# Reciprocal roots as a power on GpSimd, the B matrices on ScalarE, and another hand-made order

## The chip, the cores and the metric

The kernel runs on one core of one Trainium2 chip. Its engines work at the same time, each through its own instructions in order: TensorE (PE, with its weight loads as PEld), VectorE (DVE), ScalarE (ACT), GpSimd (POOL) and SyncE (SP), which issues the DMA transfers here. The metric is the device time of one execution in microseconds; the median of several executions is compared.

## The reference

Input is x, 16 sequences of 256 tokens of 128 values, in fp32. Four layers follow one another, each added to x after a layer norm: a Mamba layer (A), a two-deep attention-and-feed block (F), a state-space layer (C), and the same block F again with the same weights.

```python
def _layernorm(x, axis=-1, eps=1e-05):
    m = jnp.mean(x, axis=axis, keepdims=True)
    v = jnp.var(x, axis=axis, keepdims=True)
    return (x - m) / jnp.sqrt(v + eps)
...
    x = x + _L0_attn_a_ref(_layernorm(x, axis=-1), ...)   # A: conv, SSD scan, y * rsqrt(mean(y*y) + 1e-05)
    x = x + _L0_ffn_ref(_layernorm(x, axis=-1), ...)      # F
    x = x + _L0_attn_b_ref(_layernorm(x, axis=-1), ...)   # C
    x = x + _L0_ffn_ref(_layernorm(x, axis=-1), ...)      # F
```

In F, each of two depths projects q, k and v, scales q and k to length one (`t / jnp.clip(jnp.linalg.norm(t, axis=-1, keepdims=True), 1e-12)`, in 8 heads of 64), rotates them, attends in windows of 64 tokens to the own and the preceding window, projects, and then runs a layer norm and a gated feed-forward net. In C, for each of 16 states s, a recurrence runs along the tokens:

```python
        def step(state, inp):
            Ab, Bb, Bt, xt, Ct = inp
            state = Ab * state + Bb * Bt[:, None, :] * xt[:, :, None]
            out = jnp.einsum('bds,bs->bd', state, Ct)
            return (state, out)
```

followed by a layer norm of `out * z` and a projection.

## The kernel before

**Groups and stages.** Two sequences form a group (512 tokens, 4 tiles of 128), so there are 8 groups, and each goes through the stages A, F, C, F. A group's work in a stage is a unit, or six units in F: two attentions and one feed for each of two depths. In `stage` and `run` each unit gets an age, 8 times the stage plus the group, plus a little within F. In the profile below, A fills about the first 330 us, the first F runs to about 940, C to about 1600, and the second F to the end, with overlap at the borders.

**Order.** No engine's order is that of the code. A `Recorder` stands in for the machine: `add` puts each instruction of `mamba`, `attention`, `feed` and `ssm` into a `Node` with a modelled length from `lengths` and with its dependences from `touch`. `order` then plays the whole program through with these lengths: on each engine, of the nodes that could start within a small slack, it takes the one with the lowest rank. The rank is the unit's age plus the unit's entry in the table `LATE`. At most 20 units are open (6 of A, 4 of C). `order` also models table loads on ACT, a lock between POOL and some DVE instructions (`pool_end`, `both_end`), the switch of PE between tile forms (`quad`), the granted clock of PE (`HAM`, `RISE`, `FALL`), and it plans `fill` matmuls on `identb` where PE would stand still. `emit` writes the program in that order, so that each engine's order is fixed before the run.

**Buffers** come from pools (`POOLS`): 8 PSUM banks (`ps`), 47 tiles of 128x512 fp32 (`k2`) and others. A bank is taken by `mm`.

**Reciprocal roots.** `rsqrt` serves two callers. `ln_stats` calls it with `add=eps` for each layer norm, and `mamba` once more for its own norm: 96 calls in all, for 2 or 4 columns of 128 rows. They go to `rsqrt_bank`, which works on DVE in a PSUM bank: a first guess from the bits of the number, then two steps of refinement, 16 instructions, each depending on the one before or the one before that. `attention` calls `rsqrt` with `floor=1e-24` for the lengths of q and k, 32 columns, 64 calls; this is the same method in 12 POOL instructions on the tiles `rnv`, `rny`, `rnq` and `rnu`. The results go to `normalize` (DVE), to `normalize_all` (DVE for `nb`, ACT for the tiles) and, in attention, to `rotary`, which multiplies `ra` by them on POOL ahead of PE's transposes.

**The loop over states in C.** For each s of 16, `ssm` makes a matrix `b_M` for each of the group's four tiles: `self.two`, which has ones on two diagonals, times the column B of that s, a scale for each row. POOL makes all four in one instruction of 128x512, into a ring of two tiles. The row of C goes from DRAM to all partitions by an SP DMA into a ring of three (`b_r`). For each half c of the channels, ACT makes the decay by a tanh into a ring of four (`b_z`), PE multiplies `b_uT` by `b_M` into a bank, DVE adds the carry and scans along the tokens, POOL multiplies by `b_r`, and PE transposes the product and adds it up in `py`:

```python
            M = ring("b_M", s, 2, [P, NT, P])
            nc.gpsimd.tensor_tensor(M, self.two.unsqueeze(1).broadcast_to([P, NT, P]), Bt[:, :, s:s + 1].broadcast_to([P, NT, P]),
                                    ALU.mult)
```

All instructions are emitted in `emit` (L530, fillers L528), so the profile is read by tile names and not by lines. Where it says `root`, it is `rsqrt_bank`; `sm` and `pr` are the softmax, `ss` the lengths, `po` the projections.

Of the kernel before, what the change touches and what calls it, by code (L numbers as in the profile page):

```python
# [13 lines left out]
F32 = mybir.dt.float32  # L14
# [8 lines left out]
P = 128  # L23
# [18 lines left out]
NEG = -1.0e30  # L42
HCH = ((0, 128), (128, 128), (256, HID - 256))

ROWS = 3


# [3 lines left out]
       "sv": 0.08, "sg": 0.08, "gg": 0.083, "gt": 0.055, "gv": 0.035, "gs": 0.035}  # L51
TABLES = {AF.Exp: "e", AF.Tanh: "e", AF.Ln: "l", AF.Gelu: "g"}
SLOW = (AF.Tanh, AF.Ln, AF.Gelu)
HAM = 3.413
RISE, FALL = 0.53, 0.29
FILL = 0.2
POOL_SLOW = ("a_am", "a_MT", "b_av")

LATE = (1.71, -0.25, -0.97, -1.58, -0.56, 0.05, 0.77, -0.02, 1.32, 0.12, 1.03, 0.48, 0.04, 0.73, -3.9, -0.04, -1.0, -0.43, 0.8, -0.1,
        0.74, -0.48, -0.42, -1.22, 0.46, 0.57, -1.43, -1.37, -0.89, 0.25, -0.32, -0.13, -0.0, 0.04, 0.01, 0.43, -0.54, -0.18, -0.08,  # L60
        0.42, 1.15, 0.41, -0.76, -0.23, -1.37, 0.12, 0.15, -0.13, -0.45, -0.06, 0.15, 0.32, -1.79, -3.79, -1.6, 0.9, 0.04, -1.73,
        -0.17, 0.72, 0.47, 0.54, 0.44, -0.76, -0.42, 0.07, -0.71, 1.79, 1.36, 0.48, 1.05, -5.16, -2.95, 0.43, 1.03, 2.12, -0.17,
        -1.16, 0.54, 0.74, -1.96, 2.0, -0.03, 1.01, -0.93, -0.9, 1.24, 1.4, 1.4, 1.52, 2.58, 1.42, -1.22, 0.27, 2.16, 1.92, 0.34,
        -2.92, 3.73, 3.74, 1.92, 1.18, 1.54, 0.45, -1.45, 1.62, 0.87, -1.92, 0.62, -2.4, 1.87, 0.44, -1.58, -4.05, -0.49, -3.33, 2.98)
LIMIT = {"A": 6, "C": 4}
WINDOW = 20
SLACK = {"tensor": 0.0, "vector": 0.1, "scalar": 0.1, "gpsimd": 0.1, "sync": 0.0}
# [2 lines left out]
def lengths(eng, op, outs, ins, kw):  # L70

    free = lambda r: int(np.prod(r.shape[1:]))
    n = max(free(r) for r in outs + ins)
    if eng == "tensor":
        n = free(outs[0])
        if op == "transpose" or kw.get("is_transpose"):
            occ = 0.106
        elif ins[0].dt == F32:
            occ = 2 * max(0.111 * free(ins[0]) / P, 0.00084 * n)
        else:  # L80
            occ = max(0.111, 0.000452 * n)
        return occ, occ + 0.22
    aps = sum(isinstance(kw.get(k), Ref) for k in ("bias", "scale"))
    if eng == "scalar":
        occ = 0.1 + 0.000714 * n + 0.09 * aps + 0.05 * (kw.get("func") in SLOW) + 0.065 * ("accum_out" in kw)
        if outs[0].t.cls == "hT":
            occ += 0.1
        return occ, occ + 0.12
    if eng == "vector":
        n1 = n * (2 if op == "tensor_tensor_scan" else 1)  # L90
        small = sum(free(r) == 1 for r in ins) if n > 1 else 0
        two = op in ("tensor_scalar", "tensor_copy", "memset") and not any(r.t.cls == "ps" for r in outs + ins)
        occ = 0.06 + 0.00104 * n1 * (0.5 if two else 1.0) + 0.05 * small
        if outs[0].t.cls == "hT":
            occ += 0.1
        return occ, occ + 0.09
    if eng == "gpsimd":
        full = op == "tensor_tensor" and not any(r.wide for r in ins)
        per = 0.00226 if full else 0.00182 if op == "tensor_tensor" else 0.0009
        occ = 0.14 + per * n if n < 256 else 0.06 + per * n  # L100
        if outs[0].t.name.startswith(POOL_SLOW):
            occ += 0.2
        return occ, occ + 0.07
    return 0.06, 2.3


def sem(a, b):
# [71 lines left out]

class Node:  # L180
    __slots__ = ("eng", "calls", "occ", "lat", "pre", "post", "wait", "unit", "i", "table", "bufs", "new", "start", "ready", "both",
                 "quad", "fill", "took", "flow")

    def __init__(self, eng, unit, i):
        self.eng, self.unit, self.i = eng, unit, i
        self.calls, self.occ, self.lat, self.pre, self.post, self.bufs, self.new = [], 0.0, 0.0, {}, [], [], []
        self.table, self.both, self.quad, self.start, self.flow = None, False, False, None, 0.0


class Unit:  # L190
# [13 lines left out]
class Recorder:  # L204
# [10 lines left out]
        self.unit = Unit(name, age)  # L215

    @contextmanager
    def burst(self, quad=False):

        self.open = self.node("tensor")  # L220
        self.open.quad = quad
        yield
        self.open = None
# [13 lines left out]
    def add(self, eng, op, args, kw):  # L237
# [27 lines left out]
        elif eng == "tensor" and outs[0].shape[0] == 64:  # L265
            occ, lat = 0.55 * occ, 0.55 * occ + 0.22
        if eng == "tensor":
            q.flow += (2 if ins[0].dt == F32 and op == "matmul" and not kw.get("is_transpose") else 1) * int(np.prod(outs[0].shape[1:])) / 2400
        q.lat = q.occ + lat
        q.occ += occ  # L270
# [72 lines left out]
    def order(self, slack, rank, window):  # L343
# [8 lines left out]
        free = {c: [(0.0, i) for i in range(n)] for c, n in self.pools.items()}  # L352
        oldest = 0
        at = {e: 0.0 for e in self.ENGINES}
        table, quad, pool_end, both_end = None, False, 0.0, 0.0

        half, stretch, work = True, 0, 0.0
        cands = {e: [] for e in self.ENGINES}
# [78 lines left out]
        while len(done) < len(self.nodes):  # L437
# [11 lines left out]
            if e == "tensor":  # L449

                idle = t - at[e]
                bank = max((free[b.cls][0][0] for b in q.new if b.cls == "ps"), default=None)
                if FILL and idle > FILL and bank is not None and q.unit.age > -1:
                    q.fill = max(0, int((t - max(bank, at[e])) / (0.43 if half else 0.215)))
                    work += q.fill * (0.43 if half else 0.215)
                if bool(q.quad) != quad:
                    quad = bool(q.quad)
                    t += 0.09 if quad else 0.16
                while t > (stretch + 1) * HAM:
                    half = work < (RISE if half else FALL) * HAM  # L460
                    work, stretch = 0.0, stretch + 1
                if half:
                    occ, lat = 2.05 * occ, lat + 1.05 * occ
                work += q.flow * (2 if half else 1)
            if q.table:
                table = q.table
# [4 lines left out]
                pool_end = t + lat  # L471
                dirty.add("vector")
            if q.both:
                both_end = t + lat
                dirty.add("gpsimd")
            for b in q.new:
                b.place = free[b.cls].pop(0)[1]
# [39 lines left out]

    def emit(self, nc, make, idle):
        self.prepare()
        late = dict(zip(self.units, LATE))  # L520
        nodes, end = self.order(SLACK, lambda q: q.unit.age + late[q.unit], WINDOW)
        for q in nodes:
            for b in q.new:
                b.real = make(b)
# [99 lines left out]
class Kern:  # L624
# [75 lines left out]

    def rsqrt(self, x, n, tag, add=None, floor=None):


        g = self.nc.gpsimd
        k1, c1 = 0.7039522, 2.3892446
        if add is not None:
            return self.rsqrt_bank(x, n, add)
        v, y, q, u = (self.t([P, n], tag=f"{tag}{i}") for i in "vyqu")
        g.tensor_scalar(v, x, floor, None, ALU.max)
        g.tensor_scalar(y.bitcast(I32), v.bitcast(I32), -0.5, float(0x5F1FFFF9), ALU.mult, ALU.add)  # L710
        g.tensor_tensor(q, y, y, ALU.mult)
        g.tensor_tensor(q, q, v, ALU.mult)
        g.tensor_scalar(q, q, -k1, k1 * c1, ALU.mult, ALU.add)
        g.tensor_tensor(y, y, q, ALU.mult)
        g.tensor_tensor(q, y, y, ALU.mult)
        g.tensor_tensor(q, q, v, ALU.mult)
        g.tensor_scalar(u, q, 0.375, -1.25, ALU.mult, ALU.add)
        g.tensor_tensor(u, u, q, ALU.mult)
        g.tensor_scalar(u, u, 1.875, None, ALU.add)
        g.tensor_tensor(y, y, u, ALU.mult)  # L720
        return y

    def rsqrt_bank(self, x, n, add):

        g = self.nc.vector
        k1, c1 = 0.7039522, 2.3892446
        bank = self.mm("root")
        e, y, q = (bank[:, i * n:i * n + n] for i in range(3))
        v, u, r = (self.t([P, n], tag="root") for i in range(3))
        k = lambda value: self.number(value).broadcast_to([P, n])  # L730
        self.nc.after_last()
        g.memset(e, add)
        g.tensor_tensor(v, x, e, ALU.add)
        g.tensor_tensor(e, x, e, ALU.add)
        g.tensor_tensor(q, e.bitcast(I32), k(-0.5), ALU.mult)
        g.tensor_tensor(y.bitcast(I32), q, k(float(0x5F1FFFF9)), ALU.add)
        g.tensor_tensor(u, y, v, ALU.mult)
        g.tensor_tensor(q, u, y, ALU.mult)
        g.tensor_tensor(u, k(c1), q, ALU.subtract)
        g.tensor_tensor(y, y, u, ALU.mult)  # L740

        g.tensor_tensor(u, y, v, ALU.mult)
        g.tensor_tensor(q, u, y, ALU.mult)
        g.tensor_tensor(u, q, k(10 / 3 / k1 ** 2), ALU.subtract)
        g.tensor_tensor(q, u, q, ALU.mult)
        g.tensor_tensor(u, q, k(5 / k1 ** 4), ALU.add)
        g.tensor_tensor(y, y, u, ALU.mult)
        g.tensor_tensor(r, y, k(0.375 * k1 ** 5), ALU.mult)
        return r

    def number(self, value):

# [523 lines left out]
    def ssm(self, g):  # L1276
# [86 lines left out]

        for s in range(16):
            M = ring("b_M", s, 2, [P, NT, P])
            nc.gpsimd.tensor_tensor(M, self.two.unsqueeze(1).broadcast_to([P, NT, P]), Bt[:, :, s:s + 1].broadcast_to([P, NT, P]),
                                    ALU.mult)
            q = ring("b_r", s, ROWS, [P, n])
            nc.sync.dma_start(q, rows[s, :].partition_broadcast(P))
            for c in range(2):  # L1370
# [120 lines left out]
```

## Time and profile before

| | us |
|---|---|
| median of 3 runs | 2267.78 |
| range of the runs | 2260.32 to 2270.0 |
| profiled execution | 2273.8 |
| span of the profiled execution | 2272.0 |
| PE busy | 2104.1 |
| DVE busy | 1819.0 |
| POOL busy | 1642.7 |
| ACT busy | 1545.5 |
| filler matmuls on PE, busy | 147.07 |
| table loads on ACT, 84 of 1.283 us | 107.8 |

The mean granted clock of PE is 0.955 of full speed. The span is that from the first to the last instruction of the profiled execution; 1.8 us lie around it. Busy shares are means over stages that differ, so they are read by stretch. A wait is put down to the instruction that came last before the waiting one could start. The chain of waits goes back from the last instruction, at each step to what released it.

The costliest groups of POOL, as the page has them (line, engine, operation, out<-in, shapes, count | busy us, mean ns | idle before it, and what ended most of it):

```profile
L530 POOL TENSOR_TENSOR ra<-ra,rb 128x512 f32<-128x512 f32 x256 | 327.8, 1284 | 126.1 <-DVE rb L530 62.8
L530 POOL TENSOR_TENSOR b_z<-b_z,b_r 128x512 f32<-128x512 f32 x256 | 323.3, 1285 | 34.2 <-DVE b_z L530 10.6
L530 POOL TENSOR_TENSOR pr<-pr,sm 128x512 f32<-128x512 f32 x256 | 265.6, 1045 | 112.8 <-DVE sm L530 60.0
```

### The profile page before, as it was taken

Reading aid. Unit: us, or ns where it says so; the run is one execution under the profiler, and the core shown is the slowest. Engines: PE = TensorE matmul, PEld = TensorE weight load, DVE = VectorE, ACT = ScalarE, POOL = GpSimd, SP = SyncE. Lnnn points to the kernel's source line nnn. Section 1 sums busy time; section 2 is a strip of 40 time slices with the busy share of each in tenths; the row PEclk is TensorE's granted clock in tenths of the full one; section 3 lists DMA queues with packets and bytes.
Section 4 is the critical chain, followed back from the end, with each engine's and each line's share of the span. In section 5 each row is a group of like instructions: output and inputs, shape, how many; then the busy total and the mean of one; then the engine's idle time right before and its main releaser. Section 6 shows DMA issues by size and latency. Waiting matters only on the chain.

```text
span 2272.0 us, 56516 instructions
## 1 busy us (share of the span) xinstructions
PE 2104.1 (93%) x20190; PEld 1704.8 (75%) x20190; DVE 1819.0 (80%) x5840; ACT 1545.5 (68%) x4155; POOL 1642.7 (72%) x2180
## 2 busy tenths in 40 slices
PE   8899899999999999989898988899999999999999
PEld 5667567777787678778797777888777787778777
DVE  7777699877787896585999798889888859785865
ACT  5526137878778688866655756566687777879685
POOL 2424438895877695758897969988986968977593
PEclk8768799999999999999999989999999999999999
DMA  3000011000110110111221212222100101010001
GB/s 114 21 20 10 15 40 25 20 16 23 36 27 16 34 30 20 28 39 41 85 83 59 86 58 72 64 70 66 34 23 11 32 17 31 18 29 12 20 20 25
DMA packets 56520, 84.60 MB, mean 37 GB/s; under 512 B 15280, under 2 KB 20528, under 8 KB 56240
## 3 DMA queue, kind: packets, MB, share of 16 engines
q1 hardware_dynamic: 56240, 80.99, 12.5%
q8 instruction: 161, 2.64, 0.5%
q14 instruction: 119, 0.97, 0.1%
HBM read 55.53 MB, written 8.65 MB: 28 GB/s over the span
## 4 chain that ended last, share of the span: by engine, by line
PE 50%; DVE 24%; POOL 16%; ACT 6%; issue 4%; DMA 1%; SPq 0%; POOLq 0%; DVEq 0%; ACTq 0%
PE mm L530 31%; POOL ra L530 7%; PE po L530 6%; DVE b_z L530 5%; PE av L530 4%; PE sc L530 3%; PE py L530 3%; POOL pr L530 3%; DVE root L530 3%; ACT pr L530 2%; DVE rb L530 2%; DVE ra L530 2%; PE mm L528 2%; POOL b_z L530 2%; DVE ss L530 2%
## 5 line engine op out<-in xcount | busy, mean ns | idle before, releaser
L530 POOL TENSOR_TENSOR ra<-ra,rb 128x512 f32<-128x512 f32 x256 | 327.8, 1284 | 126.1 <-DVE rb L530 62.8
L530 ACT ACTIVATE pr<-sc,nm 128x128 f32<-128x128 f32 x1024 | 365.8, 395 | 32.5 <-DVE nm L530 27.8
L530 POOL TENSOR_TENSOR b_z<-b_z,b_r 128x512 f32<-128x512 f32 x256 | 323.3, 1285 | 34.2 <-DVE b_z L530 10.6
L530 POOL TENSOR_TENSOR pr<-pr,sm 128x512 f32<-128x512 f32 x256 | 265.6, 1045 | 112.8 <-DVE sm L530 60.0
L530 DVE TENSOR_TENSOR_SCAN b_z<-mm,b_z 128x256 f32<-128x256 f32 x512 | 323.4, 675 | 11.7 <-ACT b_z L530 4.2
L530 PE MATMUL mm<-b_M,b_uT 128*128 128x128 f32 x2048 | 267.1, 281 | 19.3 <-DVE mm L530 5.6
L530 ACT ACTIVATE b_z<-b_ld,b_A 128x512 f32<-128x512 f32 x256 | 178.6, 720 | 150.1 <-PE py L530 129.5
L530 PEld LDWEIGHTS mm<-b_M,b_uT 128*128 128x128 f32 x2048 | 248.5, 195 | 30.3 <-POOL b_M L530 9.4
L530 POOL TENSOR_TENSOR ra<-ra,rny 128x512 f32<-128x512 f32 x256 | 260.8, 1044 | 2.5
L530 ACT ACTIVATION_READ_ACCUMULATOR pr<-sc,nm 128x1 f32 x1024 | 239.1, 234 | 0.0
L530 DVE TENSOR_REDUCE nm<-sc 128x4 f32<-128x512 f32 x256 | 165.5, 681 | 59.1 <-PE sc L530 58.1
L530 DVE TENSOR_TENSOR rb<-mm,tab 128x256 f32<-128x256 f32 x512 | 194.9, 413 | 0.1
L530 DVE TENSOR_TENSOR ra<-mm,tab 128x512 f32<-128x512 f32 x256 | 174.2, 681 | 22.6 <-ACT sq L530 19.7
L530 ACT ACTIVATE sq<-mm 128x512 f32<-128x512 f32 x256 | 153.0, 614 | 49.7 <-PE mm L530 41.2
L530 PE MATMUL py<-ident,b_z 128*128 128x128 f32 x1024 | 157.5, 280 | 31.1 <-POOL b_z L530 30.3
L530 DVE TENSOR_REDUCE ss<-sq 128x8 f32<-128x512 f32 x256 | 172.2, 674 | 0.0
L530 PE MATMUL mm<-ident,pr 128*128 128x128 f32 x1024 | 153.2, 280 | 19.0 <-POOL pr L530 14.0
L530 PE MATMUL mm<-ident,ra 128*128 128x128 f32 x1024 | 152.6, 283 | 19.6 <-POOL ra L530 16.1
L530 ACT COPY pT<-mm 128x512 f32<-128x512 f32 x256 | 147.5, 610 | 32.0 <-PE mm L530 28.6
L530 POOL TENSOR_TENSOR b_M<-b_two,b_CB 128x512 f32<-128x512 f32 x128 | 133.8, 1055 | 31.9 <-PE mm L530 31.7
L530 PEld LDWEIGHTS py<-ident,b_z 128*128 128x128 f32 x1024 | 116.7, 142 | 52.2 <-POOL b_z L530 47.4
L530 PEld LDWEIGHTS mm<-ident,pr 128*128 128x128 f32 x1024 | 113.7, 141 | 55.7 <-POOL pr L530 39.6
(295 smaller groups left out, 5501.2 us busy)
## 6 DMA issues: line engine op xcount, KB each, us to landing
b_r<-b_rows SPq DMA_DIRECT2D x128, 256.0 KB, 3.3
v<-v SPq DMA_DIRECT2D x128, 128.0 KB, 2.2
x<-xd SPq DMA_DIRECT2D x32, 256.0 KB, 2.8
xd<-x SPq DMA_DIRECT2D x24, 256.0 KB, 2.0
x<-in_x_dram SPq DMA_DIRECT2D x16, 256.0 KB, 2.8
x<-xd SPq DMA_DIRECT2D x32, 128.0 KB, 2.4
out_dram<-x SPq DMA_DIRECT2D x16, 128.0 KB, 2.1
w<-in_wqkv_dram SPq DMA_DIRECT2D x6, 256.0 KB, 5.3
```

Source lines behind the costliest of these rows:

```text
L528: self.tc.keep_in_program_order(nc.tensor.matmul(bank[:, 0:512], idle[0], idle[1], start=True, stop=True))
L530: r = getattr(e, op)(*(a.get() if isinstance(a, Ref) else a for a in args), **{k: v.get() if isinstance(v, Ref) else v for k, v in kw.item ...
```

## The change

Three things change.

1. `rsqrt` becomes two POOL instructions for either caller: an addition (or, in attention, the maximum with the floor) and a power with exponent -0.5, both operands as tensors where the exponent is a broadcast constant. `rsqrt_bank` is gone, and with it its DVE instructions and its PSUM banks. The layer-norm roots move from DVE to POOL.
2. In `ssm`, `b_M` is made by ACT instead of POOL: four activations of 128x128 (`Identity`, with the column of B as the scale) for one POOL instruction of 128x512. `M_ACT = 4` makes the condition hold for every s.
3. The order: the modelled lengths in `lengths` change a little, PE's switch times become a table by kind of switch, some matmuls get an extra length, the lock's end is modelled otherwise, and the rank gets a second part. `LATE` has a new entry for each unit, and after these an entry for each kind of node (stage, engine and first tile name), which is added too.

The diff, with the numbers of `LATE` and some of the bookkeeping left out:

```diff
+M_ACT = 4
...
+TENSOR_SLOW = ("a_B", "a_st")
+SWITCH = {(0, 4): 0.09, (0, 2): 0.09, (4, 0): 0.16, (2, 0): 0.16, (2, 4): 0.14, (4, 2): 0.09}
 HAM = 3.413
-RISE, FALL = 0.53, 0.29
+RISE, FALL = 0.51, 0.275
...
     if eng == "scalar":
-        occ = 0.1 + 0.000714 * n + 0.09 * aps + 0.05 * (kw.get("func") in SLOW) + 0.065 * ("accum_out" in kw)
+        occ = 0.106 + 0.000714 * n + 0.09 * aps + 0.05 * (kw.get("func") in SLOW) + 0.065 * ("accum_out" in kw)
...
-        occ = 0.06 + 0.00104 * n1 * (0.5 if two else 1.0) + 0.05 * small
+        occ = 0.065 + 0.00104 * n1 * (0.5 if two else 1.0) + 0.05 * small
+        if two and small:
+            occ += 0.03
...
-        occ = 0.14 + per * n if n < 256 else 0.06 + per * n
+        occ = 0.15 + per * n if n < 256 else 0.068 + per * n
         if outs[0].t.name.startswith(POOL_SLOW):
-            occ += 0.2
+            occ += 0.1
...
+def kind(q):
+
+    return q.unit.name[0] + q.eng[0] + next(a.t.name for a in q.calls[0][1] if isinstance(a, Ref)).rstrip("0123456789")
...
+            if len(q.calls) == 0 and ins[0].t.name.startswith(TENSOR_SLOW):
+                occ, lat = occ + 0.16, lat + 0.16
+            q.slow |= ins[0].dt == F32 and not q.quad
...
-                if bool(q.quad) != quad:
-                    quad = bool(q.quad)
-                    t += 0.09 if quad else 0.16
+                if q.quad != quad:
+                    t += SWITCH[quad, q.quad]
+                    quad = q.quad
...
                 if half:
-                    occ, lat = 2.05 * occ, lat + 1.05 * occ
+                    occ, lat = 2.05 * occ, lat + 1.05 * (lat if q.slow else occ)
...
             if q.both:
-                both_end = t + lat
+                both_end = t + occ - 0.01
...
-        late = dict(zip(self.units, LATE))
-        nodes, end = self.order(SLACK, lambda q: q.unit.age + late[q.unit], WINDOW)
+        late, kinds = dict(zip(self.units, LATE)), {}
+        for q in self.nodes:
+            q.rank = q.unit.age + late[q.unit] + LATE[len(self.units) + kinds.setdefault(kind(q), len(kinds))]
+        nodes, end = self.order(SLACK, lambda q: q.rank, WINDOW)
...
     def rsqrt(self, x, n, tag, add=None, floor=None):
 
-
         g = self.nc.gpsimd
-        k1, c1 = 0.7039522, 2.3892446
+        v, y = (self.t([P, n], tag=f"{tag}{i}") for i in "vy")
+        k = lambda value: self.number(value).broadcast_to([P, n])
         if add is not None:
-            return self.rsqrt_bank(x, n, add)
-        v, y, q, u = (self.t([P, n], tag=f"{tag}{i}") for i in "vyqu")
-        g.tensor_scalar(v, x, floor, None, ALU.max)
-        g.tensor_scalar(y.bitcast(I32), v.bitcast(I32), -0.5, float(0x5F1FFFF9), ALU.mult, ALU.add)
...
-        g.tensor_tensor(y, y, u, ALU.mult)
+            g.tensor_tensor(v, x, k(add), ALU.add)
+        else:
+            g.tensor_scalar(v, x, floor, None, ALU.max)
+        g.tensor_tensor(y, v, k(-0.5), ALU.pow)
         return y
-
-    def rsqrt_bank(self, x, n, add):
-
-        g = self.nc.vector
...
         for s in range(16):
             M = ring("b_M", s, 2, [P, NT, P])
-            nc.gpsimd.tensor_tensor(M, self.two.unsqueeze(1).broadcast_to([P, NT, P]), Bt[:, :, s:s + 1].broadcast_to([P, NT, P]),
-                                    ALU.mult)
+            if s % 4 < M_ACT:
+                for i in range(NT):
+                    nc.scalar.activation(M[:, i, :], self.two, AF.Identity, scale=Bt[:, i, s:s + 1])
+            else:
+                nc.gpsimd.tensor_tensor(M, self.two.unsqueeze(1).broadcast_to([P, NT, P]), Bt[:, :, s:s + 1].broadcast_to([P, NT, P]),
+                                        ALU.mult)
```

## The prediction

> **What bounds the kernel now.** I read the busy table first, then the busy time of four stretches cut where the slices change character, then the waits of the third stretch, then the chain of waits, then the tiles that the change touches.
>
> The page's busy lines, the granted clock and the chain by engine:
>
> ```profile
> PE 2104.1 (93%) x20190; PEld 1704.8 (75%) x20190; DVE 1819.0 (80%) x5840; ACT 1545.5 (68%) x4155; POOL 1642.7 (72%) x2180
> ...
> PEclk8768799999999999999999989999999999999999
> ...
> PE 50%; DVE 24%; POOL 16%; ACT 6%; issue 4%; DMA 1%; SPq 0%; POOLq 0%; DVEq 0%; ACTq 0%
> ```
>
> PE looks full, but part of it is filler (matmuls on `identb` from L528, in the place of idling). So I cut the span at 330, 940 and 1600 us. Columns: stretch, length, busy us (instructions) of PE, PEld, DVE, ACT, POOL, clock, DMA share, GB/s; after them PE and PEld busy of the filler alone.
>
> ```profile
> 0.00:330.00 330.00, 301.71 (x1457) 205.09 (x1458) 249.89 (x911) 138.21 (x264) 115.37 (x173) 0.78 0.12 37
> 330.00:940.00 610.00, 579.36 (x6505) 461.23 (x6506) 495.89 (x1665) 481.59 (x1515) 473.87 (x727) 0.99 0.10 26
> 940.00:1600.00 660.00, 586.69 (x4976) 523.71 (x4972) 561.01 (x1625) 411.23 (x750) 549.40 (x513) 0.97 0.21 64
> 1600.00:2272.00 672.00, 636.33 (x7264) 514.73 (x7262) 512.16 (x1642) 514.45 (x1628) 504.08 (x770) 0.99 0.09 22
> ...
> 0.00:330.00 330.00, 68.19 (x250) 24.73 (x250) 0.78 0.12 37
> 330.00:940.00 610.00, 31.43 (x116) 10.51 (x115) 0.99 0.10 26
> 940.00:1600.00 660.00, 9.25 (x34) 3.28 (x34) 0.97 0.21 64
> 1600.00:2272.00 672.00, 38.20 (x135) 12.94 (x135) 0.99 0.09 22
> ```
>
> The four stretches have different limits. First (Mamba, A): DVE is busy 76%, PE does 234 us of real work and is at clock 0.78. Second and fourth (attention and feed, F): PE does 548 of 610 and 598 of 672 us. Third (SSM, C): DVE 85%, POOL 83%, PE 89%. The waits of the third stretch name the loop behind this:
>
> ```profile
> ACT b_z L530 <- PE py L530: 129.5, 109, 6.2
> PEld py L530 <- POOL b_z L530: 46.7, 70, 2.3
> POOL b_M L530 <- PE mm L530: 31.7, 9, 11.4
> PE py L530 <- POOL b_z L530: 30.3, 45, 2.1
> ```
>
> PE waits for POOL's product, ACT waits for the PE transposes that free the ring of four z tiles. POOL is the full one here, and ACT has some 150 us of waits to spare.
>
> **What is removed.** These rows hold most of it (busy, mean ns | idle before):
>
> ```profile
> L530 DVE TENSOR_TENSOR root<-root,root 128x4 f32<-128x4 f32 x448 | 71.1, 161 | 4.7
> L530 POOL TENSOR_TENSOR rnq<-rnq,rnv 128x32 f32<-128x32 f32 x128 | 32.9, 257 | 4.4
> L530 POOL TENSOR_TENSOR b_M<-b_two,b_CB 128x512 f32<-128x512 f32 x128 | 133.8, 1055 | 31.9 <-PE mm L530 31.7
> ```
>
> Layer-norm roots: all DVE rows that write `root` sum to 225.9 us over 96 calls, 2.35 us each, in a dependent series of 16. Attention roots: the ten POOL rows of `rnv, rny, rnq, rnu` sum to 192.5 us over 64 calls, 3.0 us each. b_M: 133.8 us of POOL.
>
> How much of this is on the path? I listed the chain of waits in order of time, and summed its pieces by tile and stretch:
>
> - `root` 23.9 + 12.3 + 18.3 + 5.4 = 59.9 us
> - `rn` tiles 69.2 us, of which 33.3 in the second and 33.4 in the fourth stretch
> - `b_M` 15.6 us, all in the third
>
> So 145 us of 2272 stand on the chain under names that go away.
>
> **What is added.** No row shows a power on POOL. Low end: it costs like any two-operand POOL instruction of its size, 0.26 us (the `rnq` row). High end: it does in one instruction what the twelve did, 3.0 us. The low row is the nearest (same engine, operation and shape, another ALU function); I take twice it, 0.5 us, for 128x32 and 0.3 for 128x4. With the maximum ahead (`rnv`, 0.29) an attention root is 0.8 instead of 3.0 us.
>
> The Trainium skill speaks against this: "GPSIMD Engine Reference", section 7, gives 4 cycles an element for each link of a dependent fp32 chain. A power of some 20 such links over 32 elements would, as an estimate by that page, take about 2.1 us, and the saving per attention root would be 0.6 us instead of 2.2; the forecast below would then be some 40 us later. No row here shows it.
>
> A layer-norm root becomes an addition (0.2 us, between the 0.11 of a small memset and the 0.35 of the 128x16 `a_spe`) and a power (0.3), plus one crossing to POOL, plus what POOL is still doing. One crossing is seen at 1000.20 to 1000.27 us, from DVE `y` to POOL `x`: 0.07. POOL runs pieces of 1.04 to 1.28 us and is strictly in order. Half a piece, at 72% busy, is 0.4. Together about 1.05 instead of 2.35 us. Behind the waiting `nb`, `hn` or `y` on DVE stand `rb`, `ra`, `ss` of another attention, for which ACT and POOL wait. Where the order has nothing to put there, it costs up to 1 us of DVE a call, 96 us in all, against 226 removed. It also gives back 96 PSUM bank uses, which I cost at nothing: the waits on `root` by PE that include them are already in the chain's sum.
>
> b_M on ScalarE: `s % 4 < 4` always holds, so all 128 go, each as four activations of 128x128 with one pointer scale, and no DMA or table load with them. The nearest row is `hn<-x,nb,root`, 128x128 with two pointers: four in 1.65 us, each 0.485, so 0.39 from start to start, an overlap of 0.10. One pointer fewer is 0.09 (`b_ld` with a bias 0.721, `a_th` without 0.632), so 0.30. 512 x 0.30 = 155 us of ACT; ends 0.18 (`a_ce`, 0.277 less the overlap) and 0.485 (no overlap), 92 to 248 us. ACT of the third stretch goes from 411 to 566 us of 660, and its cover is the 150 us of waits quoted. Were these gone, half of it would count, since only the M that PE waits for next is urgent. On the path I count 8 of the 15.6 us as saved. Behind an M on ACT stand the tanh of z and the exponentials of attention; before, only z products stood behind it on POOL. SP's loads of `b_r` are issued as before, three ahead.
>
> **The sum**, on the profiled execution of 2273.8 us (span 2272.0 and 1.8 around it):
>
> - roots: 59.9 / 2.35 = 25.5 calls on the chain x 1.3 = -33
> - attention roots: 69.2 / 3.0 = 23 x 2.2 = -51
> - b_M: -8
> - order: the lists of ranks and lengths rearrange all engines; nothing shows their sign. The bounds are half of the second stretch's PE idle and filler (31 + 31 us), so -31 to +31; I take 0.
>
> -92 gives 2182. The profiled execution is 6 us above the median of the runs, 2267.78, and such sums are seldom got in full, since a second chain lies close behind; I forecast **2185**.
>
> Do the engines allow it? The third stretch keeps PE 578, ACT 566, DVE 561 - 42 = 519, POOL 549 - 134 - 12 + 12 = 415; POOL stops being the limit. The second keeps DVE about 421, POOL 424, ACT 482 beside PE 548. Yes, with PE the next limit everywhere.
>
> **The rivals.**
>
> *More than the chain shows* (0.18). With POOL and DVE at 70%, PE runs at 95% from 330 us on. (548 + 577 + 598) / 0.95 = 1814, and the first stretch 330 - 13 = 317: **2131**, or about 2110 with a better order. For it: POOL `ra` is 167 us of the chain, partly a queue. Against: `pr` and `ra` remain POOL's in any case.
>
> *ACT becomes the bound of the third stretch* (0.20). It holds 40 of 84 table loads (51 us), and 566 of 660 is as dense as DVE is now; if it gains nothing and loses 25 us, only the roots elsewhere count: 13 + 10 + 24 (second stretch) + 3 + 25 (fourth) = 75, so 2273.8 - 75 + 25 = **2224**. For it: ACT is in order. Against: the 150 us of waits. A dear power within the bounds (up to 3.0 us) takes away the 51 of the attention roots and lands at the same place, about 2235 to 2250.
>
> *The power is a loop in software, and the kernel gets slower* (0.08). Place: POOL, ahead of the `ra` products that PE's transposes wait for. The gain is gone when 23 (0.29 + p) + 25.5 (0.75 + p/4) = 129 + 8, thus at p = 3.8 us for 128x32. At p = 8, POOL in the second stretch holds 474 - 90 + 32 x 8.3 + 32 x 2.2 = 720 us instead of 610, the fourth likewise: about **2490**. For it: no row has the operation. Against: the plain arithmetic of the replaced rows is near 0.25 us.
>
> *The new order takes back what the edits give* (0.04): **2268**. That the change does not do what it says is excluded for b_M by the condition, and for the roots by the code.
>
> **The numbers.** The forecast has 0.50, with its own range 2150 to 2220. 0.5% (11 us) is about what a measurement of this kernel tells from no change. Faster: 0.50 + 0.18 + 0.20 = 0.88; same 0.04; slower 0.08. The range from 2105 to 2252 leaves out the slow rival, the order's and some of the fast one's edge.
>
> **What would show it.** Right: no `root` on PSUM, DVE some 200 us less busy, POOL about 1400, ACT about 1700, pow rows of 0.3 to 0.6 us, the third stretch near 615 to 640 us, PE's filler under 147 us. Wrong: pow rows over 2 us; ACT over 93% busy in the third stretch with PE waiting for `b_M` from ACT; DVE waiting for POOL's `y` more than 60 us.

## The result, and the profile after

The changed kernel takes 2506.27 us (median of 4 runs, 2505.06 to 2507.31) beside 2266.09 for the one before: 1.1062 times as long, 95% interval 1.1036 to 1.1088. The forecast was 2185, faster. It went the other way, as the rival that had 0.08 said.

The page after, its busy lines, the granted clock and the chain by engine:

```profile
PE 2134.7 (85%) x20079; PEld 1759.6 (70%) x20079; DVE 1648.7 (66%) x4304; ACT 1681.6 (67%) x4657; POOL 1804.5 (72%) x1601
...
PEclk8779998989989898999999999899998989899989
...
PE 34%; POOL 19%; DVE 9%; ACT 7%; issue 4%; DMA 0%; POOLq 0%; ACTq 0%; DVEq 0%; SPq 0%
```

DVE fell by 170 us and ACT rose by 136, as meant. POOL, from which 326 us of work was taken, rose by 162 all the same. The clock row, nearly all 9 from 330 us on before, now dips throughout. The chain by engine adds up to 73% here, since it could be followed back only to the last three quarters of the span; in that part the tile `rny` alone holds 204 us, 8.1% of the span.

Busy time in four stretches, cut where the stages change in this run (length, PE, PEld, DVE, ACT, POOL, clock, DMA share, GB/s):

```profile
0.00:300.00 300.00, 273.34 (x1433) 189.29 (x1434) 215.34 (x601) 139.84 (x284) 149.35 (x210) 0.82 0.13 39
300.00:1040.00 740.00, 609.65 (x6393) 489.52 (x6392) 434.14 (x1171) 477.64 (x1469) 553.38 (x468) 0.91 0.08 21
1040.00:1760.00 720.00, 639.72 (x5479) 574.56 (x5476) 567.72 (x1404) 576.53 (x1360) 540.50 (x455) 0.95 0.21 61
1760.00:2504.00 744.00, 612.03 (x6785) 506.21 (x6783) 431.47 (x1129) 487.61 (x1547) 561.24 (x471) 0.92 0.07 18
```

The first power of an attention root starts at 281 us, where the first attention root of the kernel before starts at 328, so the first stretch gained. The two F stretches, 610 and 672 us before, take 740 and 744, and in them no engine is full: POOL has 75%, PE 82%. So these stretches are long by waiting and not by load.

The groups that the change made, as the page's rows (count | busy us, mean ns | idle before, and what ended it):

```profile
L554 POOL TENSOR_TENSOR rny<-rnv,number 128x32 f32<-128x32 f32 x64 | 349.4, 5461 | 3.0
L554 POOL TENSOR_TENSOR lny<-lnv,number 128x4 f32<-128x4 f32 x64 | 66.2, 1034 | 3.4
L554 POOL TENSOR_TENSOR lny<-lnv,number 128x2 f32<-128x2 f32 x32 | 23.2, 726 | 1.5
L554 ACT ACTIVATE b_M<-b_two,b_CB 128x128 f32<-128x128 f32 x512 | 168.3, 390 | 17.6 <-PE mm L554 17.4
```

The power takes 5.46 us for 32 columns, 1.03 for 4 and 0.73 for 2. And the waits of PE name where this lands (in total, times, longest):

```profile
PE mm L554 <- POOL ra L554: 217.4, 62, 10.1
PE mm L554 <- POOL pr L554: 60.7, 26, 6.0
```

PE's transposes of `ra` come after `rotary`, which comes after the power. Before the change, the two F stretches showed 5.4 and 10.0 us of waits of PE for `ra`; the first of them (330 to 940 us):

```profile
PE mm L530 <- POOL ra L530: 5.4, 8, 1.6
```

### The profile page after: what moved, and what is told of

Read it like the earlier page. It is cut to its first block, busy times and chain, and to the rows that moved or that the text cites. A ratio compares the mean times of both kernels' runs of the same rounds, so it can differ in the third digit from the quotient of the medians.

```text
span 2504.0 us, 54715 instructions
## 1 busy us (share of the span) xinstructions
PE 2134.7 (85%) x20079; PEld 1759.6 (70%) x20079; DVE 1648.7 (66%) x4304; ACT 1681.6 (67%) x4657; POOL 1804.5 (72%) x1601
## 4 chain that ended last, share of the span: by engine, by line
PE 34%; POOL 19%; DVE 9%; ACT 7%; issue 4%; DMA 0%; POOLq 0%; ACTq 0%; DVEq 0%; SPq 0%
PE mm L554 21%; POOL rny L554 8%; POOL ra L554 6%; PE po L554 4%; PE py L554 4%; PE sc L554 2%; POOL pr L554 2%; PE av L554 2%; ACT pr L554 2%; DVE b_z L554 2%; DVE rb L554 1%; DVE ra L554 1%; DVE ss L554 1%; PE mm L552 1%; DVE nm L554 1%
## 5 line engine op out<-in xcount | busy, mean ns | idle before, releaser
L554 PE MATMUL mm<-ident,ra 128*128 128x128 f32 x1024 | 197.4, 337 | 222.8 <-POOL ra L554 216.5
L554 POOL TENSOR_TENSOR rny<-rnv,number 128x32 f32<-128x32 f32 x64 | 349.4, 5461 | 3.0
L554 PEld LDWEIGHTS mm<-ident,ra 128*128 128x128 f32 x1024 | 147.9, 173 | 264.5 <-POOL ra L554 245.7
L554 DVE TENSOR_TENSOR_SCAN b_z<-mm,b_z 128x256 f32<-128x256 f32 x512 | 318.5, 673 | 11.9 <-ACT b_z L554 4.1
L554 PE MATMUL mm<-ident,pr 128*128 128x128 f32 x1024 | 166.9, 295 | 65.6 <-POOL pr L554 60.4
L554 ACT COPY kT<-mm 128x512 f32<-128x512 f32 x128 | 76.6, 598 | 212.4 <-PE mm L554 212.1
L554 ACT ACTIVATE b_z<-b_ld,b_A 128x512 f32<-128x512 f32 x256 | 178.8, 718 | 41.1 <-PE py L554 36.5
L554 DVE TENSOR_TENSOR y<-y,po 128x128 f32<-128x128 f32 x256 | 71.4, 281 | 184.4 <-PE po L554 182.2
L554 PEld LDWEIGHTS mm<-ident,pr 128*128 128x128 f32 x1024 | 124.9, 150 | 94.6 <-POOL pr L554 76.8
```

The lines of the kernel that those rows point to most:

```text
L554: r = getattr(e, op)(*(a.get() if isinstance(a, Ref) else a for a in args), **{k: v.get() if isinstance(v, Ref) else v for k, v in kw.item ...
```

## The experiments

The theory was that the power's price is the whole loss, and that the rest of the change is as forecast. The rivals were the new order, the B matrices on ScalarE, and a variant of the first: not the length of the power costs, but that the order was laid out for a shorter one.

### One part undone, one part alone

**The series back in attention**, all else as changed:

```diff
-        g.tensor_tensor(y, v, k(-0.5), ALU.pow)
+        g.tensor_scalar(y.bitcast(I32), v.bitcast(I32), -0.5, float(0x5F1FFFF9), ALU.mult, ALU.add)
...
+        g.tensor_tensor(y, y, u, ALU.mult)
```

> The changed kernel with one part undone: the attention roots are again the series of twelve POOL instructions (3.0 us a call) and not maximum and power (0.29 + 5.46 us); layer-norm roots, B matrices and order stay as changed. Theory 1, the price of the power: the 246 us that the power and its maximum hold on the chain of waits fall to about 70, and the rest of the change brings what was forecast, so the time falls by 250 to 310 us, to 2190 to 2260. Theory 2, the new order or the B matrices on ScalarE are to blame as well: the time stays over 2300, since a good part of the loss has nothing to do with these calls.

2354.1 us, ratio 1.0405 (1.0373 to 1.0437). 152 us come back, but the kernel is still slower than before. By the number this is Theory 2. But the run changes more than one part: with other instructions the planner lays out every engine anew, with ranks that were found for another program and with a false length for the layer-norm powers. So it can't say what of the 2354 is due to the order, and the runs with the order held still, further below, speak against Theory 2.

**Only the planner learns the length**, the work is as changed:

```diff
+        if kw.get("alu") == ALU.pow:
+            occ = 0.37 + 0.159 * n
```

> The changed kernel, where only the planner learns the length of the power, 0.37 us + 0.159 us a column as the trace shows it, instead of 0.21 us for 32 columns; the program does the same work in another order. Theory 1a, the price itself (POOL is held 5.46 us, in order, ahead of products that PE waits for): the time falls by less than 60 us and stays over 2440. Theory 1b, the surprise (the order was laid out for 0.21 us, so that PE comes to the transposes 5 us early each time): the time falls by most of the 240 us, to under 2330, since POOL is only 75% busy and there is other work to put in front.

2376.19 us, 1.0504 (1.0466 to 1.0541): 130 us less than the change, between the two. In its trace PE waits only 4.2 us directly for the chain from `rny` to `ra`, and the clock is 0.965. So a good part of the loss is the surprise; but these ranks too were found for another program, and what remains cannot be put down to the price alone.

**The power alone in the old kernel**:

```diff
-        g.tensor_scalar(y.bitcast(I32), v.bitcast(I32), -0.5, float(0x5F1FFFF9), ALU.mult, ALU.add)
...
-        g.tensor_tensor(y, y, u, ALU.mult)
+        g.tensor_tensor(y, v, k(-0.5), ALU.pow)
```

> The kernel before with one part of the change alone: the attention roots as maximum and power on POOL, with the old ranks and the planner's old lengths. Theory 1: the power is enough to lose time in any order; 64 calls become 2.7 us longer each and are planned at 0.2 us, so that the time rises to 2400 to 2550. Theory 2, the new order is to blame: it stays within 1% of 2266.

2628.93 us, 1.1617 (1.1573 to 1.1661), more than expected. The power loses time without anything of the new order; Theory 1 holds, with a size above its range.

**The B matrices on ScalarE alone in the old kernel**:

```diff
-            nc.gpsimd.tensor_tensor(M, self.two.unsqueeze(1).broadcast_to([P, NT, P]), Bt[:, :, s:s + 1].broadcast_to([P, NT, P]),
-                                    ALU.mult)
+            for i in range(NT):
+                nc.scalar.activation(M[:, i, :], self.two, AF.Identity, scale=Bt[:, i, s:s + 1])
```

> The kernel before with one part of the change alone: the B matrices by four activations each on ScalarE, with the old ranks and lengths. The forecast: the third stretch gets shorter, POOL is relieved of 134 us there and ACT takes 155 us in its waits, so the time falls by 8 us by the chain of waits and by up to 45 us by the engines' loads: 2220 to 2258. The rival, ACT becomes the bound of the third stretch: 2270 to 2300.

2274.68 us, 1.0062 (1.0036 to 1.0087): a small loss. The tile view tells more than the time (duration ns min/median/max, first and last start us); first the kernel before:

```profile
L530 POOL TENSOR_TENSOR b_M<-b_two,b_CB x128: 1039/1050/1277, 941.7 to 1598.9; 128x512 f32<-128x512 f32 x128
```

and this run:

```profile
L530 ACT ACTIVATE b_M<-b_two,b_CB x512: 384/387/545, 932.3 to 1552.9; 128x128 f32<-128x128 f32 x171
```

The last B matrix is made 46 us earlier, but from there to the end of the span it is 717 us and not 673. So what is gained ahead of the last B matrix is lost behind it. That the old ranks are the reason is not shown by this run.

### The order held still

These runs have each engine's instructions in exactly the order of the kernel that they start from; only the operation of an instruction differs, and so its length. This is the cleanest test here.

**No power at all** in the changed kernel, and then the layer-norm powers back:

```diff
-        g.tensor_tensor(y, v, k(-0.5), ALU.pow)
+        g.tensor_tensor(y, v, k(1e-6), ALU.mult)
```

```diff
-        g.tensor_tensor(y, v, k(-0.5), ALU.pow)
+        g.tensor_tensor(y, v, k(-0.5), ALU.pow if floor is None else ALU.subtract)
```

> The changed kernel with its order untouched, instruction for instruction; only the operation of the 160 power instructions is a multiplication by 1e-6, so that no reciprocal root is computed. Theory 1, the price of the power is the whole loss and the rest of the change is as forecast: 2150 to 2225, below the kernel before. Theory 2, the order, the B matrices on ScalarE or the move of the layer-norm roots to POOL cost time by themselves: 2270 or more, as undoing the attention roots alone (2354) would suggest.

> As the run without any power, in the same untouched order, but the 96 layer-norm powers (1.03 and 0.73 us) are computed; the 64 attention powers are a subtraction, so that q and k are not scaled by their reciprocal lengths. Theory 1 with the whole loss in attention: within 15 us of the run without any power. Theory 1b, the layer-norm powers cost too (some 0.85 us each more than planned, a quarter of them on the path): 20 to 60 us more than that run. The sum of both steps must give 2506.

2093.56 us without any power, 0.9219 (0.917 to 0.9268), and 2133.39 with those of the layer norms, 0.9381 (0.9332 to 0.9429). The first is below the range expected, so the rest of the change is worth more than forecast. The 96 layer-norm powers cost 40 us, though they hold POOL for 68 us more than the multiplications in their place (90 and 22 us), so part of that is covered. The row of the larger ones without power, beside the 66.2 us of the changed kernel:

```profile
L554 POOL TENSOR_TENSOR lny<-lnv,number 128x4 f32<-128x4 f32 x64 | 14.6, 228 | 3.4
```

The 64 in attention cost the rest, 2506 - 2133 = 373 us, 5.8 us each, though each is only 5.2 us longer than the subtraction in its place (median 5.44 against 0.24). PE's waits for `ra` over the whole span, 217.4 us in the changed kernel, are these without the attention powers:

```profile
PE mm L554 <- POOL ra L554: 5.7, 12, 0.9
```

One place shows how. The changed kernel, POOL and then PE in order of time (start us, us, instruction, idle before):

```profile
465.01 5.42 POOL L554 TENSOR_TENSOR rny<-rnv,number 128x32 f32<-128x32 f32 x1
470.39 0.19 POOL L554 TENSOR_TENSOR lnv<-lnmv,number 128x2 f32<-128x2 f32 x1
470.55 2.04 POOL L554 TENSOR_TENSOR ra<-ra,rny 128x512 f32<-128x512 f32 x2
...
464.52 1.06 PE L554 MATMUL po<-wo,oT 128*128 128x128 f32 x8
471.64 1.11 PE L554 MATMUL mm<-ident,ra 128*128 128x128 f32 x4 [6.07 <-POOL ra L554]
```

The same instructions in the run where attention has no power:

```profile
430.58 0.24 POOL L554 TENSOR_TENSOR rny<-rnv,number 128x32 f32<-128x32 f32 x1
430.77 0.19 POOL L554 TENSOR_TENSOR lnv<-lnmv,number 128x2 f32<-128x2 f32 x1
430.93 4.05 POOL L554 TENSOR_TENSOR ra<-ra,rny 128x512 f32<-128x512 f32 x4
...
430.05 1.06 PE L554 MATMUL po<-wo,oT 128*128 128x128 f32 x8
432.02 0.66 PE L554 MATMUL mm<-ident,ra 128*128 128x128 f32 x4 [0.91 <-POOL ra L554]
```

PE's wait goes from 0.91 to 6.07 us, by the 5.2 us that the power is longer, since nothing else stands before the transposes in PE's order. And after the wait the same four transposes take 1.11 us and not 0.66. Both show in the sums over the whole span, of the change and of the run without attention powers (PE first, clock third from the end):

```profile
0.00:2504.00 2504.00, 2134.74 (x20079) 1759.59 (x20079) 1648.68 (x4304) 1681.62 (x4657) 1804.48 (x1601) 0.91 0.12 34
```

```profile
0.00:2132.40 2132.40, 2028.66 (x20079) 1677.57 (x20079) 1642.53 (x4304) 1671.01 (x4657) 1472.90 (x1601) 0.97 0.14 40
```

With the same 20079 instructions PE is busy 106 us longer, at the lower clock, and stands still 369 instead of 104 us. So of the 372 us between the spans, 265 are waiting and 106 are longer matmuls at the lower clock that came with the waiting. POOL itself is busy 332 us longer, so about a fifth of what the powers added was covered, and the clock cost more than that.

**The last of the twelve a power**, in the old kernel:

```diff
-        g.tensor_tensor(y, y, u, ALU.mult)
+        g.tensor_tensor(y, y, u, ALU.pow)
```

> The kernel before with its order untouched, instruction for instruction; only the last of the twelve POOL instructions of an attention root is a power and not a multiplication, so that the scale of q and k is off a little. It adds 64 x 5.2 us to POOL, 333 us, in the old order. Theory 1, a power ahead of the products that PE waits for costs nearly its length in any order that was laid out without it: 2470 to 2600. Theory 2, the loss is special to the new order: under 2400.

2607.51 us, 1.1468 (1.1441 to 1.1495): 5.25 us more for each of 64 calls, against the kernel before at 2271 beside it, 5.46 us being the length of the power in that trace too. That is 8 us above the range of Theory 1; Theory 2 is out.

```profile
L530 POOL TENSOR_TENSOR rny<-rny,rnu 128x32 f32<-128x32 f32 x64 | 349.8, 5465 | 2.6
PE 2203.0 (85%) x20190; PEld 1791.3 (69%) x20190; DVE 1819.3 (70%) x5840; ACT 1554.1 (60%) x4155; POOL 1979.8 (76%) x2180
```

Beside the profile of the kernel before, PE stands still 403 instead of 168 us and is busy 99 us longer, with the clock at 0.904 instead of 0.955. So it is the same loss, in the same two parts, in another order.

**The old ranks in the changed kernel without power**:

```diff
...
-            q.rank = q.unit.age + late[q.unit] + LATE[len(self.units) + kinds.setdefault(kind(q), len(kinds))]
+            q.rank = q.unit.age + late[q.unit] + 0.0
```

> As the run without any power (2094; the multiplication by 1e-6 stands for the 160 roots), but with the ranks of the kernel before: its list for the units, and nothing added by kind of node. Lengths, work and engines are as changed, so that only the order differs. The forecast took the new order at 0, within 31 us either way. Theory A, the ranks are worth little and the relief of DVE and POOL brought the 178 us: 2075 to 2125. Theory B, the ranks are worth as much as the forecast missed, some 60 to 110 us: 2155 to 2205, near the forecast of 2185.

2179.87 us, 0.9633 (0.9605 to 0.9661). This is Theory B. The new ranks bring another 86 us, to 2094; PE's busy share goes from 94% to 96% with it (old ranks, then new ones):

```profile
PE 2051.5 (94%) x20200; PEld 1690.5 (78%) x20200; DVE 1635.6 (75%) x4304; ACT 1686.5 (77%) x4661; POOL 1404.4 (64%) x1601
```

```profile
PE 2006.1 (96%) x20079; PEld 1668.1 (80%) x20079; DVE 1637.3 (78%) x4304; ACT 1668.9 (80%) x4657; POOL 1406.5 (67%) x1601
```

### Ranks made for each program

Two of the runs above, with the series back and with the length known, were slower than their work explains: both had ranks found for another program, and the first a false length for the layer-norm powers. So here the planner was told the length of the layer-norm powers, first with the ranks as they were:

```diff
+        if kw.get("alu") == ALU.pow:
+            occ = 0.37 + 0.159 * n
...
+        g.tensor_scalar(y.bitcast(I32), v.bitcast(I32), -0.5, float(0x5F1FFFF9), ALU.mult, ALU.add)
...
+        g.tensor_tensor(y, y, u, ALU.mult)
```

> The changed kernel with the attention roots as the series of twelve again and the planner told the length of the layer-norm powers (0.37 us + 0.159 us a column). Against the run with the series alone (2354) it shows what is lost there by the false length of the layer-norm powers. If much: under 2300. If little, and the ranks of the new order do not fit a program with other instructions: 2310 to 2360.

2245.21 us, 0.988 (0.9854 to 0.9906): 109 us less than with the false length (2354), and below the kernel before. That is more than the 68 us by which these powers are longer, so the plan as a whole came out better too. Then new ranks were searched for each of three programs with the kernel's own planner, longer for the last two; only the numbers of the two lists change, and in the last the B matrices:

```diff
-M_ACT = 4
+M_ACT = 0
```

> The run with the series of twelve in attention, known length of the layer-norm powers and B matrices on ScalarE (2245), with ranks laid out anew for just this program by the kernel's own planner. If the rest of the change is sound and only the attention power and ranks made for another program were in the way: 2130 to 2190, below both kernels. If the price of the roots on POOL keeps it up: over 2220.

> The change itself, both powers computed, with the planner told the power's length and the ranks laid out anew for that, by the same planner and with more effort than for the series (2187). Theory 1a, the price: even an order made for the power cannot hide 64 x 5.75 us of POOL, 368 us against 192 for the series, and the time stays over 2266, some 80 to 170 us above the series with fitted ranks: 2270 to 2360. Theory 1b, the surprise alone: within 40 us of the series, under 2230.

> The kernel with the series in attention, known length of the layer-norm powers and fitted ranks (2187), but with the B matrices on POOL again and the ranks laid out anew for that, with more effort. The forecast's term for the B matrices was -8 us by the chain of waits and up to -45 by the loads: if the move to ScalarE is worth that once the order is made for it, this run takes 2195 to 2240. If it is worth nothing (as in the old order, where it cost 0.6%): 2170 to 2190.

- the series in attention, powers in the layer norms, B on ScalarE: 2187.04 us, 0.9661 (0.9638 to 0.9685)
- the change itself, both powers: 2325.8 us, 1.0258 (1.0233 to 1.0283)
- as the first, B on POOL: 2225.12 us, 0.9818 (0.9797 to 0.984)

The first beats both kernels. The second is the fairest trial of the power: in an order made for it, it is still slower than the kernel before and 139 us behind the series. PE hardly waits for it any more:

```profile
PE mm L545 <- POOL ra L545: 10.8, 16, 3.9
```

But in place of the waits the planner put filler; the filler's busy time, of the series and of the power:

```profile
sum 2700.00, PE 123.33 PEld 41.83; mean PE 123.33 PEld 41.83
```

```profile
sum 2700.00, PE 281.82 PEld 105.71; mean PE 281.82 PEld 105.71
```

That is 158 us more filler for 137 us more span. The planner found no other work to put in front; that there is none in any order is not shown. The third says that B on ScalarE is worth some 38 us where the order is made for it, provided that two searches for the same program differ by less, which no run measured.

## Why the prediction was wrong, point by point

The way from the kernel before to the changed one, each step by a run (the kernel before, measured beside them, lay between 2261 and 2271): 2266 before; 2180 with the relief of DVE and POOL, the old ranks and powers at the price of a multiplication; 2094 with the new ranks; 2133 with the layer-norm powers; 2506 with the attention powers. By the ratios to the kernel before, which ran beside each, these steps are -83, -94, +37 and +381 us, which is the same account. The second step also holds the change's new modelled lengths; no run separates these from the relief.

**The step that failed** is the price: "The low row is the nearest (same engine, operation and shape, another ALU function); I take twice it, 0.5 us, for 128x32 and 0.3 for 128x4." It is 5.46 and 1.03 us. So the term of -51 us for the attention roots had the wrong sign: a call became 2.75 us longer and not 2.2 shorter, on POOL and ahead of what PE waits for. Of the signs of being wrong that were named, "pow rows over 2 us" is the one that was seen. The high end, 3.0 us, was no bound at all: what another method of computing a root costs in twelve instructions says nothing about a power. "GPSIMD Engine Reference", section 7, of the Trainium skill pointed the right way with its 4 cycles an element on a dependent fp32 chain. The estimate made from it, 2.1 us, was 2.6 times too small; its 20 links were a guess, and no run shows how many a power has, or whether it is such a chain. The estimate was set aside for the nearest row, which was the poorer guide.

**The slow rival's size** failed too. Its formula gives, at 5.46 and 1.03 us, 23 x 5.75 + 25.5 x 1.78 - 137 = +40 us, about 2314. It counted the 23 calls that stood on the chain before. With the order held still, the 64 calls cost 5.8 us each on average, 4.1 of them as PE standing still and 1.7 by the clock: most calls off the old chain delay PE as well when they grow twentyfold. The clock was in none of its terms. That its 2490 lies near 2506 is luck: it was meant for a power of 8 us and a full POOL, and POOL is busy only 553 of 740 us in the first F stretch. Of the 413 us that all the powers cost in this order (2094 to 2506), 180 go away when the order is made for them (2506 to 2326).

**The relief** came out as summed: -92, and -81 measured with the old ranks beside the kernel before (2261 to 2180). Some luck is in it, since the powers there cost 0.23 to 0.25 and not the 0.3 to 0.5 us assumed. That DVE would lose some 200 us (it lost 170), that ACT would reach about 1700 (1682) and POOL about 1400 without a dear power (1406) held as well.

**The order** was taken at 0, with bounds of 31 us, "half of the second stretch's PE idle and filler". It brought 86 us. The ranks act on all four stretches, whose idle and filler time is 168 and 147 us, so the bound was too narrow. The rival "more than the chain shows", 2131, expected PE at 95% from the freed engines. These alone left it at 94% over the span and 2180; 96% and 2094 came with the new ranks.

**B on ScalarE** was priced at 0.30 us a piece; seven in a row take 2.14 us with 0.39 for one, 0.29 from start to start. Its term of -8 us was +14 in the old order (1.0062) and -38 between fitted ones; the -45 by the engines' loads, which the prediction does not have but the expectations of two runs, was the nearer there. ACT did not become the bound: its waits for PE's `py` in the third stretch went from 129.5 to 36.5 us, and it is busy 577 of 720 us there.

**The layer-norm roots** were to wait on DVE for up to 1 us a call. The waits of DVE for `lny` come to 54 us in all (26.8 for `hn`, 11.9 for `nb`, 8.0 for `x`, 7.2 for `y`), below the 60 that were named as a sign of error; the powers behind them cost 40 us of time.

**Small slips** change nothing: the parts named for a layer-norm root, 0.2, 0.3, 0.07 and 0.4, add up to 0.97 and not 1.05 us (2 us in the sum), and the 10 in the sum of the ScalarE rival is the third stretch's, where the second's, 7, was meant (2227 instead of 2224).

What stays open is how far longer searches would lower the three fitted kernels, and how much the time scatters from one search to the next. That POOL's share of the loss could be had back by a root on another engine was not tried.

## What to carry to other kernels

An instruction that no row shows has no price from its shape: another operation of the same engine and form can be twenty times as long, and one run of it is worth more than any bound. In a program whose order is fixed beforehand, a wrong length can cost at most calls and not only at those on the old chain: here the 64 attention calls cost a little more than the length that was added, clock included, and the 96 shorter ones 40 of 68 us. To price one operation there, exchange it for a cheap one and leave the order as it is; to compare two programs, lay out the order for each, since the same edit cost 0.6% with ranks made without it and brought some 1.7% with ranks made for it.

## What the runs showed of the hardware that was not expected

A power on POOL grows with the columns, 0.158 us for each: medians of 0.70 us for 2, 1.01 for 4 and 5.44 for 32 columns of 128 rows, on a line that is about 0.37 us at none, where a multiplication of 32 columns takes 0.25. The time hardly varies (5.40 to 6.16 us over 64 calls, the median the same in the order that was made for it). DVE is not held for that long: its longest instruction takes 1.81 us in the changed kernel and 1.80 in the one before.
